# A four-layer graph network kernel: LSTM state laid batch-outer again, attention as a two-deep pipeline over groups

## The chip, the cores and the metric

The kernel runs on one core of a Trainium2 chip. The core has five engines that run side by side, each through its own queue: TensorE (PE for its matmuls, PEld for its weight loads), VectorE (DVE), ScalarE (ACT), GpSimd (POOL) and SyncE (SP, which only issues transfers here). They wait for each other through semaphores. The metric is the device time of one execution in microseconds (us). A profile gives, for one execution, the start and length of each instruction and the clock that was granted to TensorE, as a share of full speed.

## The reference

The input is x, 128 graphs of 64 nodes with 256 features in fp32: 8192 tokens. One 64x64 matrix adj serves all graphs. Four layers follow each other; each normalizes x over its features, applies ReLU, computes a function of the result and adds it to x.

```
layer 0: h = relu(adj (h Wg0 + bg0)); h = relu(adj (h Wg1 + bg1))
         for p in 1, 2, 3, 4:                    # windows of p nodes
             wins = h[:, : (64 // p) * p] as windows of p nodes
             h at the last node of each window = last hidden state of an
                 LSTM (weights of p, gates i, f, g, o) over the window
layer 1: attention with 4 heads of 64 features over the 64 nodes of a graph,
         scores masked where adj == 0
layer 2: normalized adj times h, two linear layers, each with a batch norm
layer 3: three graph convolutions with adj * adj, 256-512-1024-256
```

The four LSTMs run one after another, since each reads what the one before wrote into h.

## The kernel before

**Tiling.** The 8192 tokens are 16 groups of 512 (GN); x stays in SBUF in 16 tiles, xs[g], tokens on partitions. Matmuls are fp32; the program's records show two TensorE instructions for each written matmul (transposes one). All PSUM results go through one ring of eight banks (bank(), L49).

**Layer 0.** For each group (L192 to L209), the graph convolutions leave features on partitions, tokens along the free dimension. ScalarE writes the result into one of four resident tiles hs[i], each for 32 graphs (HB). A tile is [P, 2, NODES, HB]: the node is the outer index and the graph the inner one, so ScalarE reads its PSUM bank with a step of 64 elements (L207). The LSTM stage (L211 to L311) works on blocks of up to 512 windows, two blocks at a time. gate() (L222) multiplies the input of step t, read straight from hs (`win`, L218), and from step 1 on the hidden state `hid`, by the gate's weights, accumulates in one bank, and ScalarE applies sigmoid or tanh (L235). VectorE combines the gates into the cell (L245 to L250) and the new hidden state; at a window's last step the product is written back into hs (L258). What a matmul streams at step t is

```
hw = hs[i][:, :, k0 * p : (k0 + nk) * p, b0 : b0 + nb]
win = [hw[:, c].rearrange("p (k q) b -> p k q b", q=p) for c in range(2)]
... win[c][:, :, t, :]                  # runs of nb = 32 or 16 neighbours
```

to_residual (L269) first copies a group from hs into graph-outer order (hc; one half by POOL, one by VectorE, L275), then TensorE transposes it and VectorE adds it to x (L288). For the first two tiles this is issued in the middle of the LSTM with p = 4, for the other two after it.

**Layer 1.** For each group in turn (L319 to L409): ln_relu and to_features give hT; eight matmuls give queries and keys (L332, copied by ScalarE at L336), then values (L347, L353); 32 matmuls of 64x64 give the scores (L363); VectorE scales and masks them (L369), subtracts the maximum (L376, L377), ScalarE takes the exponential (L378), VectorE the sum and its reciprocal; TensorE transposes the result (L388), ScalarE copies it to eT (L391), 32 matmuls of 64x64 multiply it by the values (L399), VectorE divides by the sum (L406) and POOL adds to x (L409). A 64x64 matmul uses a quarter of the array: `par` selects the half of the rows (where its operands lie), `b` the half of the columns (where its output goes). In the loops of L356 to L362 and L393 to L398, par is the outermost index.

**Layers 2 and 3** follow with the lines L441 to L568; the change doesn't touch them.

**Order.** The program is written as above; a scheduler then puts each engine's instructions into one fixed queue, and may move some ahead, above all layer-norm statistics (L113, L115) of later groups. Engines take their queues strictly in order. Pools with bufs=2 let two groups' tiles live at the same time.

## Time and profile before

Median of three runs: 3057.72 us (3055.09 to 3057.88).

| | us |
|---|---|
| profiled execution, own time | 3057.72 |
| its span, first to last instruction | 3055.9 |
| TensorE matmul busy | 2908.4 (95%) |
| VectorE, ScalarE, POOL busy | 880.1, 860.4, 126.9 |
| mean TensorE clock | 0.964 |

Cut by stages, from the start of each to the start of the next:

| stage | from, us | length, us | TensorE clock |
|---|---|---|---|
| setup and graph convolutions | 0.0 | 234.9 | 1.00 |
| LSTM p=1 | 234.9 | 164.7 | 1.00 |
| LSTM p=2 | 399.6 | 302.0 | 1.00 |
| LSTM p=3 | 701.6 | 343.5 | 1.00 |
| LSTM p=4, half of the residual | 1045.1 | 381.6 | 1.00 |
| rest of the residual, first norm | 1426.7 | 17.2 | 1.00 |
| attention | 1443.9 | 407.6 | 0.77 |
| layer 2, first half | 1851.5 | 161.8 | 0.96 |
| layer 2, second half | 2013.3 | 145.7 | 0.96 |
| layer 3 | 2159.0 | 896.9 | 1.00 |

In the profile's lines L12 is line 12 of the kernel; a group names engine, operation, output<-inputs, shape and count, then busy time and mean length of one in ns, then the engine's idle time before it and what ended it. A matmul's length overlaps with the next one's, so the distance of starts says more than the length. "h" in a matmul of L230 is the tile hs, "hid" the hidden state.

### The profile page before, as it was taken

Reading aid. Unit: us, or ns where it says so; the run is one execution under the profiler, and the core shown is the slowest. Engines: PE = TensorE matmul, PEld = TensorE weight load, DVE = VectorE, ACT = ScalarE, POOL = GpSimd, SP = SyncE. Lnnn points to the kernel's source line nnn. Section 1 sums busy time; section 2 is a strip of 40 time slices with the busy share of each in tenths; the row PEclk is TensorE's granted clock in tenths of the full one; section 3 lists DMA queues with packets and bytes.
Section 4 is the critical chain, followed back from the end, with each engine's and each line's share of the span. In section 5 each row is a group of like instructions: output and inputs, shape, how many; then the busy total and the mean of one; then the engine's idle time right before and its main releaser. Section 6 shows DMA issues by size and latency. Waiting matters only on the chain.

```text
span 3055.9 us, 28553 instructions
## 1 busy us (share of the span) xinstructions
PE 2908.4 (95%) x12130; PEld 1727.2 (57%) x12130; DVE 880.1 (29%) x1789; ACT 860.4 (28%) x1435; POOL 126.9 (4%) x122
## 2 busy tenths in 40 slices
PE   7999999999999999999888888999999999999999
PEld 6784444446666544444555555544565656656656
DVE  5332222222222212434433435444521211111111
ACT  2324533333333322322323326260311111111111
POOL 1000000000000000101111112000000000000000
PEclk9999999999999999999777778999999999999999
DMA  5000000000000000000000000001000000000000
GB/s 163 1 1 0 1 14 0 1 0 28 1 1 1 14 0 0 0 0 25 1 1 1 1 1 1 0 1 48 1 14 7 14 7 7 14 7 8 14 7 14
DMA packets 23938, 32.35 MB, mean 11 GB/s; under 512 B 1281, under 2 KB 20225, under 8 KB 23809
## 3 DMA queue, kind: packets, MB, share of 16 engines
q1 hardware_dynamic: 22512, 29.63, 2.9%
q8 instruction: 95, 1.56, 0.2%
q10 hardware_dynamic: 1296, 0.89, 0.1%
q14 instruction: 35, 0.28, 0.0%
HBM read 22.13 MB, written 8.39 MB: 10 GB/s over the span
## 4 chain that ended last, share of the span: by engine, by line
PE 91%; DVE 4%; ACT 2%; POOL 1%; issue 1%; DMA 0%; ACTq 0%; POOLq 0%; DVEq 0%
PE ps L230 39%; PE ps L541 14%; PE ps L555 7%; PE ps L140 5%; PE ps L332 4%; PE ps L529 4%; PE ps L475 4%; PE ps L451 3%; PE ps L181 3%; PE ps L347 2%; PE ps L399 2%; PE ps L130 1%; PE ps L363 1%; PE ps L388 1%; PE ps L563 1%; POOL rstd L117 1%
## 5 line engine op out<-in xcount | busy, mean ns | idle before, releaser
L230 PE MATMUL ps<-h,w 128*128 128x512 f32 (+1 forms) x2016 | 809.1, 541 | 0.0
L230 PEld LDWEIGHTS ps<-h,w 128*128 128x128 f32 x2016 | 382.8, 190 | 377.5 <-issue 298.7
L230 PE MATMUL ps<-hid,w 128*128 128x512 f32 (+1 forms) x1152 | 466.3, 527 | 0.0
L541 PE MATMUL ps<-arena 128*128 128x512 f32 x1024 | 442.1, 592 | 0.0
L230 PEld LDWEIGHTS ps<-hid,w 128*128 128x128 f32 x1152 | 218.7, 190 | 199.5 <-issue 150.4
L541 PEld LDWEIGHTS ps<-arena 128*128 128x128 f32 x1024 | 193.3, 190 | 237.3 <-issue 236.5
L555 PE MATMUL ps<-arena 128*128 128x256 f32 x1024 | 223.6, 379 | 0.0
L555 PEld LDWEIGHTS ps<-arena 128*128 128x128 f32 x1024 | 194.6, 190 | 33.3 <-issue 7.7
L249 DVE TENSOR_TENSOR gi<-gi,gg 128x512 f32<-128x512 f32 (+1 forms) x72 | 43.9, 610 | 438.1 <-ACT gg L235 438.1
L235 ACT ACTIVATE gg<-ps,lbias 128x512 f32<-128x512 f32 (+1 forms) x144 | 91.9, 638 | 235.2 <-PE ps L230 235.2
L548 DVE TENSOR_SCALAR arena<-ps 128x512 f32<-128x512 f32 x64 | 44.3, 692 | 391.7 <-PE ps L541 391.7
L235 ACT ACTIVATE gi<-ps,lbias 128x512 f32<-128x512 f32 (+1 forms) x144 | 91.9, 638 | 219.4 <-PE ps L230 219.4
L546 ACT ACTIVATE arena<-ps 128x512 f32<-128x512 f32 x64 | 38.2, 597 | 404.5 <-PE ps L541 404.5
L332 PE MATMUL ps<-hT,wqk 128*128 128x512 f32 x256 | 133.7, 682 | 1.4 <-DVE rstd L116 1.4
L253 ACT ACTIVATE th<-c 128x512 f32<-128x512 f32 (+1 forms) x144 | 83.6, 581 | 157.3 <-DVE c L250 105.7
L451 PE MATMUL ps<-arena,w 128*128 128x512 f32 x256 | 116.5, 609 | 8.9 <-DVE arena L446 8.9
L475 PE MATMUL ps<-arena,w 128*128 128x512 f32 x256 | 112.8, 604 | 5.2 <-ACT arena L467 5.2
L529 PE MATMUL ps<-arena 128*128 128x512 f32 x256 | 115.0, 602 | 0.4 <-DVE arena L524 0.4
L245 DVE TENSOR_TENSOR c<-gi,gg 128x512 f32<-128x512 f32 (+1 forms) x72 | 46.9, 651 | 199.1 <-ACT gg L235 199.1
L117 POOL TENSOR_TENSOR rstd<-rstd,mhalf 128x4 f32<-128x4 f32 x64 | 64.5, 1008 | 891.7 <-DVE rstd L116 891.7
L140 PEld LDWEIGHTS ps<-wT,arena 128*128 128x128 f32 x768 | 93.3, 195 | 12.3 <-issue 7.7
L388 PE MATMUL ps<-ident,e 128*128 128x128 f32 x128 | 31.5, 428 | 71.0 <-ACT e L378 71.0
(114 smaller groups left out, 2629.5 us busy)
## 6 DMA issues: line engine op xcount, KB each, us to landing
x<-in_x SPq DMA_DIRECT2D x16, 512.0 KB, 9.1
out<-x SPq DMA_DIRECT2D x16, 512.0 KB, 2.9
w<-in_wih SPq DMA_DIRECT2D x4, 1024.0 KB, 8.7
w<-in_whh SPq DMA_DIRECT2D x3, 1024.0 KB, 5.7
arena<-in_l3w SPq DMA_DIRECT2D x3, 1024.0 KB, 5.0
wg<-in_wg ACTq DMA_DIRECT2D x2, 256.0 KB, 4.3
wqk<-in_wqkv SPq DMA_DIRECT2D x1, 512.0 KB, 3.7
w<-in_w1t SPq DMA_DIRECT2D x1, 512.0 KB, 4.9
```

What stands on the lines that cost most here:

```text
L117: nc.gpsimd.tensor_tensor(out=rstd, in0=rstd, in1=mhalf, op=ALU.pow)
L140: nc.tensor.matmul(ps[:, t * P : (t + 1) * P], lhsT=src[:, t, c * P : (c + 1) * P], rhs=rhs, start=True, stop=True,)
L181: nc.tensor.matmul(ps[:, t, :], lhsT=srcT[:, c, tok : tok + P], rhs=w[:, c, :], start=(c == 0), stop=(c == 1),)
L230: nc.tensor.matmul(o, lhsT=lhsT, rhs=rhs, start=(k == 0), stop=(k == len(ops) - 1))
L235: nc.scalar.activation(g[:, 0:n], ps, func, bias=lbias[:, col : col + 1])
L253: nc.scalar.activation(th[:, 0:n], cm, AF.Tanh)
L332: nc.tensor.matmul(ps, lhsT=wqk[:, c, col : col + P], rhs=hT[:, c, :], start=(c == 0), stop=(c == 1),)
L451: nc.tensor.matmul(ps, lhsT=w1[:, c, m * P : (m + 1) * P], rhs=a[:, 2 + c, :], start=(c == 0), stop=(c == 1),)
L475: nc.tensor.matmul(ps, lhsT=w2[:, c, m * P : (m + 1) * P], rhs=a[:, c, :], start=(c == 0), stop=(c == 3),)
L529: nc.tensor.matmul(ps, lhsT=a[:, 2 + c, t * P : (t + 1) * P], rhs=w31[:, c, :], start=(c == 0), stop=(c == 1),)
L541: nc.tensor.matmul(ps, lhsT=w32[k][:, c, m * P : (m + 1) * P], rhs=m1[:, c, :], start=(c == 0), stop=(c == 3),)
L555: nc.tensor.matmul(ps[:, t, :], lhsT=h2[c // 4][:, c % 4, tok : tok + P], rhs=w33[:, c, :], start=(c == 0), stop=(c == 7),)
```

## The change

Two parts. In layer 0, hs is [P, 2, HB * NODES]: the graph is the outer index and the node the inner one. The input of step t is then read, and the window's result written, with a step of p elements. hs is already in the order that the residual needs, so the copies hc are gone; the transposes and adds of all groups come after the last LSTM. ScalarE writes hs from PSUM in plain order. The blocks are cut by graphs alone; the numbers and sizes of the matmuls stay the same.

In layer 1 the body is cut into functions (features, queries_keys, values, softmax, turn, attend), and the loop runs one group ahead: the transposition of the softmax and the product with the values belong to the group before the one whose queries, keys, values and scores are computed. In both 64x64 passes par becomes the innermost index and each par has its own bank, so that consecutive matmuls use the four quarters of the array in turn.

```diff
-            hres.tile([P, 2, NODES, HB], F32, tag=f"h{i}", name=f"h{i}")
+            hres.tile([P, 2, HB * NODES], F32, tag=f"h{i}", name=f"h{i}")
...
-                        dst[:, c], ps.rearrange("p (b n) -> p n b", n=NODES), AF.Relu
+                mix(s1, adjT, 2, lambda c, ps: nc.scalar.activation(dst[:, c, :], ps, AF.Relu))
...
-                hw = hs[i][:, :, k0 * p : (k0 + nk) * p, b0 : b0 + nb]
-                win = [hw[:, c].rearrange("p (k q) b -> p k q b", q=p) for c in range(2)]
+                hb = hs[b0 // HB].rearrange("p c (b n) -> p c b n", n=NODES)
+                hb = hb[:, :, b0 % HB : b0 % HB + nb, 0 : nw * p]
+                win = [
+                    hb[:, c].rearrange("p b (k q) -> p b k q", q=p) for c in range(2)
+                ]
...
-                    ops = [(wi[:, c, col : col + P], win[c][:, :, t, :]) for c in range(2)]
+                    ops = [(wi[:, c, col : col + P], win[c][:, :, :, t]) for c in range(2)]
...
-            def to_residual(i):
-                    hc = lp.tile([P, 2, GB, NODES], F32, tag="hc", name="hc")
-                    for c, eng in enumerate((nc.gpsimd, nc.vector)):
-                        eng.tensor_copy(
-                            hc[:, c], hs[i][:, c, :, b0 : b0 + GB].rearrange("p n b -> p b n")
-                        )
...
-            for p, nk, nb in ((1, 16, 32), (2, 16, 32), (3, 21, 16), (4, 16, 32)):
+            for p, nb in ((1, 8), (2, 16), (3, 16), (4, 32)):
...
-                        if p == 4 and j == 2 and t < 2:
-                            to_residual(t)
-            for i in range(2, len(hs)):
-                to_residual(i)
+            for g in range(NG):
+                per = HB * NODES // GN
+                hsrc, o = hs[g // per], (g % per) * GN
+                for k in range(2):
...
+            pss = [bank((P, 2 * GT, NODES)) for _ in range(2)]
+            for t in range(GT):
+                for m in range(2):
                     for b in range(2):
                         tok = t * P + b * NODES
-                        for m in range(2):
+                        for par in range(2):
+                            rows = slice(par * 64, par * 64 + 64)
                             nc.tensor.matmul(
-                                ps[b * 64 : b * 64 + 64, 2 * t + m, :],
+                                pss[par][b * 64 : b * 64 + 64, 2 * t + m, :],
...
+        last = None
+        for g in range(NG + 1):
+            if g < NG:
+                hT = features(g)
+                q, k = queries_keys(hT)
+            if last is not None:
+                e, ri, v_last = last
+                eT = turn(e)
+            if g < NG:
+                v = values(hT)
+            if last is not None:
+                attend(g - 1, eT, v_last, ri)
+            if g < NG:
+                last = (*softmax(q, k), v)
```

## The prediction

> **What bounds the kernel now.** I first cut the span into stages (the busy time by stretches; columns: stretch, its length, busy time and instructions of PE, PEld, DVE, ACT, POOL, then granted clock, DMA share, GB/s):

> ```profile
> 399.60:701.60 302.00, 302.00 (x705) 133.72 (x704) 65.50 (x97) 95.56 (x145) 0.00 (x0) 1.00 0.01 4
> 701.60:1045.10 343.50, 343.50 (x1217) 231.02 (x1216) 80.06 (x160) 115.54 (x224) 0.00 (x0) 1.00 0.02 6
> 1045.10:1426.70 381.60, 378.77 (x929) 170.87 (x929) 106.69 (x201) 101.71 (x153) 15.04 (x13) 1.00 0.01 3
> ...
> 1443.90:1851.50 407.60, 336.41 (x3576) 242.11 (x3576) 160.33 (x317) 121.99 (x202) 54.78 (x47) 0.77 0.01 4
> ```

> The first three are the LSTMs of window 2, 3 and 4: TensorE is busy without a gap at full clock, so every nanosecond added to a matmul there is added to the time. The last is attention: TensorE idles 71 us, and its clock averages 0.77. Next I read one attention group in TensorE's timeline (start, length):

> ```profile
> 1489.74 3.27 PE L399 MATMUL ps<-v,eT 64*64 64x64 f32 x62
> 1492.94 1.97 PE L130 MATMUL ps<-ident,h 128*128 128x128 f32 x8
> 1494.83 8.98 PE L332 MATMUL ps<-hT,wqk 128*128 128x512 f32 x16
> 1503.74 3.76 PE L347 MATMUL ps<-wv,hT 128*64 128x128 f32 x64
> 1507.43 2.00 PE L363 MATMUL ps<-k,q 64*64 64x64 f32 x64
> 1513.88 1.97 PE L388 MATMUL ps<-ident,e 128*128 128x128 f32 x8 [4.45 <-ACT e L378]
> 1515.78 3.43 PE L399 MATMUL ps<-v,eT 64*64 64x64 f32 x64
> ```

> The wait of 4.45 us is for the softmax, and it costs a second time: the same 64 matmuls take 2.00 us before it (L363) and 3.43 us after it (L399). Stretches cut at these passes show clock 0.50 for L388, L399 and L130 and 1.00 for L347 and L363. Groups alternate between 25.0 and 26.2 us, 25.6 on average. Last, the groups by form, for what strided reads show:

> ```profile
> L230 PE MATMUL ps<-h,w 128*128 128x512 f32 x1312 | 589.3, 592 | 0.0
> L230 PE MATMUL ps<-h,w 128*128 128x336 f32 x704 | 219.8, 446 | 0.0
> ...
> L275 POOL COPY hc<-h 128x512 f32<-128x512 f32 x16 | 18.8, 1201 | 1248.9 <-DVE h L258 1123.3 <-PE ps L284 125.6
> ...
> L275 DVE COPY hc<-h 128x512 f32<-128x512 f32 x16 | 8.9, 598 | 0.1
> ```

> A matmul's 592 ns includes overlap; the spacing is what counts. In the timeline four 128x512 records start every 1.715 us (429 ns each) and four 128x336 every 1.13 us (282 ns). Check: the 384+704 records of windows 1 and 2 times 429 ns are 466.7 us, exactly their stretch, and 1216 times 282.5 ns are the 343.5 us of window 3. One element passes each 0.84 ns. L275 is the only element-wise strided SBUF read on VectorE (step 128 bytes).

> [...]

> **Part A, the LSTM layout.** Instruction counts and sizes are unchanged. The moving operand's inner step becomes p elements (L225): 4 bytes at p=1, 8 at p=2, 12 at p=3, 16 at p=4. Only the input product (names h,w) is affected; hid stays contiguous. Records: 384 at p=1, 448 at p=2, 704 at p=3, 480 at p=4. TensorE's price is unknown and bounded thus. Low end 0[...]. Middle[...]. Then p=2[...] costs nothing; p=3 touches three lines per four elements[...], 433 against 282 ns; p=4 costs 880 against 429 ns. That is 704 x 0.149 = 105 plus 480 x 0.447 = 214, together **+319 us**. High end:[...] p=2 pays 448 x 0.447 = 200 and p=3 704 x 0.293 = 206, together +620. I take the middle[...]. Nothing hides it, TensorE being full.

> VectorE's last products (L258) now write with the same steps. At most 40 of them, 0.69 us each, may take twice as long; VectorE is under 30% busy there, so this hides under the matmuls, except for the last, some 0.5 us.

> **Part B, the residual after the LSTM.** Gone: 16 POOL and 16 VectorE copies (L275), and 2.8 us in which TensorE waited for them inside window 4. But all 128 transposes and 32 adds (L288) now stand after the last LSTM matmul. Adds bind: 32 x 0.625 = 20 us, done 21.5 us after that matmul; stats, aggregate, rstd on POOL (1.0), relu: 4.5; remaining relus, transposes, copies to hT: 3.5. First query matmul at 29.5. Before: 17.2, plus the 64 transposes (7.6 us) and 2.8 us of waiting inside window 4, is 27.6. **+2 us.**

> **Part C, the pipeline.** The queued order is now: turn (the transposes of L388) of group g-1 after queries/keys of g, then values, attend of g-1, scores of g. Before each score evacuation VectorE has nothing late; after it, it copies the two halves of the next hT with the maximum between. From the end of scores, by the durations above at full clock:
> - two e (1.50), first hT half (0.69): 2.4; maximum (1.22), second half (0.69): 4.4. TensorE has transposes (0.96, half of 1.97) and two records in that time, so it idles some 2.5 us, in two pieces, below what cost it the clock before.
> - 14 more L332 records at 0.429: 10.4. The softmax is done at 6.7 (subtract 1.23, exponential 1.06), so turn doesn't wait: 11.4.
> - values 3.7: 15.1; attend and scores, 64 records each, 30.5 ns now at full clock. Going round four quarters[...] 1.6 us each: 18.3. If rotation brings nothing, 19.0.

> 14 cycles x (25.6 - 18.3) = **-102 us**. The first two groups gain nothing: VectorE has some 19 us of statistics for later groups queued ahead of the first e, which holds the scores' readers until about 48 us after the LSTM where scores end at 44. The last group drains as before.

> Sum against the profiled span: 3055.9 + 319 + 2 - 102 = 3274.9. The profiled execution's own time is 1.8 above its span and is also the median of the three runs, so **3277 us**.

> **Rivals.**
> - *TensorE doesn't mind the step (faster).* Part A costs 0: 3057.7 + 2 - 102 = 2958 us. For it: TensorE streams at 0.84 ns per element[...], so a line per element may be just enough; ScalarE reads PSUM with a 256-byte step at L206 (595 ns) as quickly as contiguously at L200 (594).[...] It decides at p=4: if p=3 is free, break-even is a record of 429 + 100/0.48 = 637 ns, 1.24 ns per line.
> - *Only 16 bytes pays.*[...] 3277 - 105 = 3172 us.
> - *The pair rule.* p=2 and p=3 pay in full: 3277 + 301 = 3578 us.
> - *The pipeline gives little.* VectorE's order (maximum ahead of the second hT half) or the ring of eight PSUM banks leaves cycles at 22 us: a gain of 50, so 50 us more in each case above.

> **How the numbers follow.** Full line cost 0.31 (3277); no cost 0.27 (2958); only p=4 0.22 (3172); pair rule or worse 0.14 (3578); a smaller mixture, mostly under 100 us, 0.06. A difference within 0.2%, 6 us, is no more than measurements of this kernel tell from no change. Faster 0.27 and a little of the mixture, 0.29; same 0.02; slower 0.69. The range 2945 to 3330 leaves out only the pair rule and a few worse tails. The likeliest's own range, with the pipeline at 75 to 115 us, is 3235 to 3330.

> **What would show it.** The h,w records' spacing: 429 ns at p=1 and p=2, 433 at p=3, 880 at p=4, beside unchanged hid records. Window 4's stretch should grow by 211, window 3's by 105. In attention: clock near 1.0, cycles near 18.3, no wait of the turn (L388) for the exponential. Wrong if p=4 records stay at 429, if p=2 records lengthen, or if the clock stays at 0.5 behind each score pass.

## The result and the profile after

The changed kernel takes **3274.17 us** (median of four runs, 3272.86 to 3277.01), beside 3057.03 us for the kernel before in the same comparison: a ratio of 1.0712 (95% interval 1.0694 to 1.0731), 217 us slower. The predicted time was 3277 us. The total hides two errors of about 35 us with opposite signs, so the parts have to be read one by one.

The first view is again the busy time by stretches, now of the kernel after (stretch, length, busy time and instructions of PE, PEld, DVE, ACT, POOL, then clock, DMA share, GB/s), cut where the LSTMs with p = 2, 3 and 4, the residual and attention begin:

```profile
399.30:710.60 311.30, 311.30 (x705) 132.44 (x704) 65.43 (x97) 95.66 (x145) 0.00 (x0) 1.00 0.01 4
710.60:1172.70 462.10, 462.10 (x1217) 236.20 (x1216) 81.29 (x160) 118.72 (x225) 0.00 (x0) 1.00 0.01 5
1172.70:1769.40 596.70, 596.70 (x865) 172.31 (x864) 79.42 (x112) 102.52 (x152) 0.00 (x0) 1.00 0.01 2
1769.40:1797.75 28.35, 18.89 (x137) 14.75 (x135) 25.94 (x62) 4.24 (x8) 2.01 (x2) 0.87 0.21 66
1797.75:2067.60 269.85, 240.18 (x3576) 165.91 (x3576) 155.02 (x357) 118.63 (x203) 54.79 (x47) 0.97 0.01 2
```

TensorE is busy throughout the three LSTM stretches, as before, with as many instructions, and yet they are longer: 302.0 has become 311.3, 343.5 has become 462.1. Window 4 before was 381.6 us, of which some 370.7 were its 864 matmul records and 10.9 half of the residual; it is now 596.7 without any residual. Attention went from 407.6 to 269.85 us and its clock from 0.77 to 0.97.

| part | predicted | measured in the profiles |
|---|---|---|
| LSTM p=2 | 0 | 311.3 - 302.0 = +9.3 |
| LSTM p=3 | +105 | 462.1 - 343.5 = +118.6 |
| LSTM p=4 | +214 | 596.7 - 370.7 = +226.0 |
| residual | +2 | 28.35 - 17.2 - 10.9 = +0.3 |
| attention | -102 | 269.85 - 407.6 = -137.8 |

These add up to +216.4, and the spans differ by 217.0 (3272.9 and 3055.9).

The matmuls that became longer are those that read hs. TensorE's timeline of the kernel after at p = 3 and at p = 4 (start, length of the merged stretch; it is the distance of starts that counts):

```profile
799.73 1.97 PE L227 MATMUL ps<-h,w 128*128 128x336 f32 x4
801.53 1.30 PE L227 MATMUL ps<-hid,w 128*128 128x336 f32 x4
802.67 1.97 PE L227 MATMUL ps<-h,w 128*128 128x336 f32 x4
...
1400.22 1.90 PE L227 MATMUL ps<-hid,w 128*128 128x512 f32 x4
1401.96 3.76 PE L227 MATMUL ps<-h,w 128*128 128x512 f32 x4
1405.54 1.90 PE L227 MATMUL ps<-hid,w 128*128 128x512 f32 x4
```

At p = 3 four h records take 1.80 us and four hid records, of the same size but contiguous, 1.14: 450 and 285 ns each. At p = 4 it is 3.58 and 1.73 us: 895 and 433 ns. The same reading at p = 2 (502.13 to 503.93 us) gives 450 against 429 ns, and at p = 1 the records stay at 429.

Attention, one group of the kernel after in TensorE's timeline (L393 is the product with the values, L350 the scores, L313 the queries and keys, L379 the transposition of the softmax):

```profile
1835.54 7.11 PE L313 MATMUL ps<-hT,wqk 128*128 128x512 f32 x16 [1.20 <-DVE hT L131]
1842.48 1.04 PE L379 MATMUL ps<-ident,e 128*128 128x128 f32 x8
1843.44 3.76 PE L330 MATMUL ps<-wv,hT 128*64 128x128 f32 x64
1847.14 1.16 PE L393 MATMUL ps<-v,eT 64*64 64x64 f32 x64
1848.12 1.11 PE L350 MATMUL ps<-k,q 64*64 64x64 f32 x64
1849.16 1.09 PE L128 MATMUL ps<-ident,h 128*128 128x128 f32 x8
1851.58 0.67 PE L313 MATMUL ps<-hT,wqk 128*128 128x512 f32 x1 [1.32 <-DVE hT L131]
```

The wait for the exponential is gone. What is left is 1.3 us per group before the query and key matmuls, for the copy to hT. A cycle is 1851.58 - 1835.54 = 16.04 us, against 25.6 before. The pass with the values takes 0.98 us from its start to the next start, where it had been 3.36. The scores' pass takes 1.04 us; as a stretch it is 1.11 us long and was 2.00.

### The profile page after: what moved, and what is told of

Same layout as the page of the kernel before. It is cut to its first block, busy times and chain, and to the rows that moved or that the text cites. A ratio compares the mean times of both kernels' runs of the same rounds, so it can differ in the third digit from the quotient of the medians.

```text
span 3272.9 us, 28518 instructions
## 1 busy us (share of the span) xinstructions
PE 3165.4 (97%) x12130; PEld 1662.9 (51%) x12130; DVE 858.6 (26%) x1773; ACT 860.9 (26%) x1435; POOL 107.7 (3%) x106
## 4 chain that ended last, share of the span: by engine, by line
PE 91%; DVE 5%; ACT 2%; POOL 1%; issue 0%; DMA 0%; ACTq 0%; POOLq 0%; DVEq 0%
PE ps L227 47%; PE ps L552 13%; PE ps L566 7%; PE ps L138 4%; PE ps L540 3%; PE ps L486 3%; PE ps L313 3%; PE ps L462 3%; PE ps L179 2%; PE ps L330 2%; POOL rstd L115 1%; PE ps L574 1%; DVE st L111 1%; ACT h L118 1%; PE ps L393 1%; DVE x L288 1%
## 5 line engine op out<-in xcount | busy, mean ns | idle before, releaser
L227 PE MATMUL ps<-h,w 128*128 128x512 f32 (+1 forms) x2016 | 1162.3, 721 | 0.0
L227 PEld LDWEIGHTS ps<-h,w 128*128 128x128 f32 x2016 | 390.7, 194 | 587.8 <-issue 546.0
L313 PE MATMUL ps<-hT,wqk 128*128 128x512 f32 x256 | 117.1, 611 | 25.1 <-DVE hT L131 25.1
L232 ACT ACTIVATE go<-ps,lbias 128x512 f32<-128x512 f32 (+1 forms) x144 | 91.1, 633 | 96.6 <-PE ps L227 94.4
L232 ACT ACTIVATE gf<-ps,lbias 128x512 f32<-128x512 f32 (+1 forms) x72 | 44.8, 623 | 231.8 <-PE ps L227 231.8
```

Source lines behind the costliest of these rows:

```text
L227: nc.tensor.matmul(o, lhsT=lhsT, rhs=rhs, start=(k == 0), stop=(k == len(ops) - 1))
L232: nc.scalar.activation(g[:, 0:n], ps, func, bias=lbias[:, col : col + 1])
L313: nc.tensor.matmul(ps, lhsT=wqk[:, c, col : col + P], rhs=hT[:, c, :], start=(c == 0), stop=(c == 1),)
```

## The experiments

**One part at a time.** The first question was whether the two parts are what they seem: each was taken alone, by joining the layer 0 of one kernel to the attention of the other.

The pipeline alone is the kernel before with the whole of the change in layer 1, the round of the four quarters included; these are its first and last lines:

```diff
-        for g in range(NG):
+        def features(g):
             h = ap_.tile([P, GT, D], F32, tag="h", name="h")
             ln_relu(xs[g], h)
             hT = ap_.tile([P, 2, GN], F32, tag="hT", name="hT")
             to_features(h, hT)
+            return hT
...
+        last = None
+        for g in range(NG + 1):
```

> The layout of before with the pipelined attention. If the two parts add up, attention falls from 407.6 to about 270 us as in the changed kernel and the LSTM stages stay at 164.7, 302.0 and 343.5 us: 3057 - 137 = 2920 us. Rival: part of the attention's gain was owed to the new layout (group 0's statistics, residual order); then the attention stage stays above 280 us and the time above 2930 us.

Measured: 2913.70 us, ratio 0.9535 (0.9521 to 0.9549), 141 us faster.

The layout alone is the kernel before with the change in layer 0:

```diff
-            hres.tile([P, 2, NODES, HB], F32, tag=f"h{i}", name=f"h{i}")
+            hres.tile([P, 2, HB * NODES], F32, tag=f"h{i}", name=f"h{i}")
...
-                    ops = [(wi[:, c, col : col + P], win[c][:, :, t, :]) for c in range(2)]
+                    ops = [(wi[:, c, col : col + P], win[c][:, :, :, t]) for c in range(2)]
```

> The layout of the changed kernel with the attention of before. If the two parts add up: LSTM 1535 us instead of 1181 without its residual, attention near 408 us: 3274 + 137 = 3411 us. Rival: the two parts interact (statistics or residual adds that now collide with attention): off by more than 10 us from 3411.

Measured: 3415.23 us, ratio 1.1177 (1.1160 to 1.1194), 360 us slower. The two differences, +360.1 and -141.4 against their common reference of 3055.12, add up to +218.7, and the change as a whole is +217.1. So the parts hardly interact. In the pipeline alone, attention takes 261.5 us rather than 269.85, since there the statistics of the first groups are done earlier (the second group's matmuls wait 0.97 us for hT, and 5.43 us in the changed kernel) and the first group runs at full clock (its query and key matmuls take 7.03 us, and 8.59 in the changed kernel). This is where it beat its expectation by 6 us.

**What a strided read costs TensorE.** Three prices had to be told apart: one for every line (a line is here 16 bytes of SBUF, counted from the tile's start), one for every element outside an aligned pair (the prediction's pair rule), one by the step. The 450 ns at p = 2, where no two streamed words are neighbours, already speak against the second; but the changed kernel varies lines and step together. So the next kernel streams runs of two neighbouring words, placed differently at each window size.

```diff
+# per window size: first word, words in a run, words from run to run
+PATTERNS = {2: (1, 2, 4), 3: (0, 2, 6), 4: (3, 2, 8)}
...
+                    off, run, hop = PATTERNS[p]
+                    v = flat[:, c, 0 : n // run * hop].rearrange("p (r s) -> p r s", s=hop)
+                    return v[:, :, off : off + run]
...
-                    ops = [(wi[:, c, col : col + P], win[c][:, :, :, t]) for c in range(2)]
+                    ops = [(wi[:, c, col : col + P], src(c, t)) for c in range(2)]
```

> The changed kernel with other words streamed into the input products (the LSTMs compute with other inputs; counts and sizes stay): p=2 runs of two words, words 1 and 2 of each four; p=3 words 0 and 1 of each six; p=4 words 3 and 4 of each eight, which lie on both sides of a line's border. If a 16-byte line costs about 1.75 ns whatever is read of it: p=2 450 ns per record (one line per pair), p=3 295 ns, p=4 895 ns (each word its own line), total about 3274 - 704 x 0.155 = 3165 us. If only pairs that start on an 8-byte border run at full speed: p=2 and p=4 895 ns, p=3 283 to 295 ns, about 3360 us. If the step of the innermost dimension decides (4 bytes everywhere): 429, 283 and 429 ns, about 2930 us.

Measured: 3164.41 us in its one run, beside 3165 by the line rule. TensorE's timeline of this kernel at p = 3 and at p = 4:

```profile
875.69 1.34 PE L243 MATMUL ps<-h,w 128*128 128x336 f32 x4
876.87 1.29 PE L243 MATMUL ps<-hid,w 128*128 128x336 f32 x4
877.99 1.34 PE L243 MATMUL ps<-h,w 128*128 128x336 f32 x4
...
1301.15 1.90 PE L243 MATMUL ps<-hid,w 128*128 128x512 f32 x4
1302.88 3.76 PE L243 MATMUL ps<-h,w 128*128 128x512 f32 x4
1306.46 1.90 PE L243 MATMUL ps<-hid,w 128*128 128x512 f32 x4
```

At p = 3 four h records take 1.18 us, 295 ns each; at p = 4 3.58 us, 895 ns each; at p = 2 they stand at 450 ns. All three are what the line rule gives. The aligned-pair rule falls with p = 2, whose pairs start off an 8-byte border and cost no more than a step of two words does; a rule by the step falls with p = 4, where neighbouring words that lie on both sides of a line's border cost as much as words 16 bytes apart.

The next kernel asks whether the distance between lines counts, and whether a broken run costs anything by itself.

```diff
-PATTERNS = {2: (1, 2, 4), 3: (0, 2, 6), 4: (3, 2, 8)}
+PATTERNS = {2: (0, 4, 8), 3: (0, 3, 4), 4: (0, 1, 8)}
...
+                    if p == 4:
+                        line = flat[:, c].rearrange("p (r s) -> p r s", s=hop)[:, :, off]
+                        return line.unsqueeze(1).to_broadcast([P, 2, n // 2])
```

> The changed kernel with other words streamed into the input products (the LSTMs compute with other inputs; counts and sizes stay): p=2 runs of four words on a line, every second line; p=3 three words of each four; p=4 one word of each eight, 32 bytes apart, swept twice. If a line costs 1.75 ns however far the next one is: 429 ns (four words per line), 283 ns, 895 ns, total 3274 - 9 - 118 = 3147 us. Rival, the step's size matters beyond 16 bytes[...]: p=4 above 895 ns[...]. Rival, any break in the run costs: p=2 and p=3 above 429 and 283 ns.

Measured: 3154.07 us in its one run. Its timeline at p = 4:

```profile
1299.15 3.83 PE L246 MATMUL ps<-h,w 128*128 128x512 f32 x4
1302.80 1.90 PE L246 MATMUL ps<-hid,w 128*128 128x512 f32 x4
1304.54 3.83 PE L246 MATMUL ps<-h,w 128*128 128x512 f32 x4
```

Four records take 3.65 us, 912 ns each: 32 bytes apart costs 2% more than 16. So the size of the step counts, as that rival says, but little; larger distances were not run. That the words are swept twice is not the cause: the kernel after this one sweeps words 16 bytes apart four times, and its records start every 0.90 us, as they do inside a run of four of the changed kernel. These 17 ns on 480 records are 8 us, the miss against the expectation. Runs of four on every second line stand at 429 ns (1.71 us for four, at p = 2), and three words of each four at 283 ns: in these two patterns, of 128 and 112 lines per record, a broken run costs nothing.

The last of this group measures whether the price belongs to TensorE's clock. In the attention of before, the first 1.4 to 3.8 us of a group's query and key matmuls run at half clock (0.50 from 1521.04 to 1522.40 us and, one group earlier, from 1494.83 to 1498.6); there they were made to stream one word of each line.

```diff
+            sparse = [
+                hT[:, c].rearrange("p (r s) -> p r s", s=4)[:, :, 0]
+                .unsqueeze(1).to_broadcast([P, 4, GN // 4])
+                for c in range(2)
+            ]
...
-                            ps, lhsT=wqk[:, c, col : col + P], rhs=hT[:, c, :],
+                            ps.rearrange("p (a r) -> p a r", a=4),
+                            lhsT=wqk[:, c, col : col + P], rhs=sparse[c],
```

> The kernel before, with the query and key matmuls streaming one word of each 16-byte line of hT, swept four times (the attention computes with other queries and keys). The first some 4 us of these matmuls run at half clock in every group, the rest at full clock. If the time per line belongs to the memory and not to TensorE's clock: all 16 records stand at 895 ns. If it is counted in TensorE's cycles: 895 ns at full clock, twice that, 1790 ns, at half clock. Total for the first: 16 x 0.895 = 14.3 us instead of 7.7 to 8.9 per group, 3057 + 16 x 6.0 = 3153 us; for the second about 1.8 us more per group, 3182 us.

Measured: 3158.69 us in its one run. TensorE's timeline, one group:

```profile
1505.67 1.97 PE L130 MATMUL ps<-ident,h 128*128 128x128 f32 x8
1507.57 14.75 PE L337 MATMUL ps<-hT,wqk 128*128 128x512 f32 x16
1522.24 3.77 PE L353 MATMUL ps<-wv,hT 128*64 128x128 f32 x64
```

The 16 records take 1522.24 - 1507.57 = 14.67 us. The next view has first the stretch of this group that ran at half clock (the third number from the end), then weight loads, one of which starts with each record from the second on:

```profile
1507.57:1510.20 2.63, 2.63 (x4) 1.11 (x4) 0.86 (x2) 2.08 (x4) 0.27 (x2) 0.50 0.00 0
...
1508.63 0.31 PEld L337 LDWEIGHTS ps<-hT,wqk 128*128 128x128 f32 x1 [0.57 <-DVE hT L133]
1509.54 0.31 PEld L337 LDWEIGHTS ps<-hT,wqk 128*128 128x128 f32 x1 [0.59 <-issue]
1510.43 0.21 PEld L337 LDWEIGHTS ps<-hT,wqk 128*128 128x128 f32 x1 [0.59 <-issue]
```

The second record, at half clock, takes 0.90 us, and so does each of those that follow at full clock (1510.43 is the start of the fourth); only the first takes 1.07 us. Counted in TensorE's cycles, the second would have taken 1.79 us. So the time per line is not counted in TensorE's cycles. The half clock covered less of these matmuls than the "some 4 us" of the expectation, here 2.6 us, but that doesn't change the reading.

All together, with the lines that a record touches:

| read | lines per record | ns per record | ns per line |
|---|---|---|---|
| p=4, one word per line (mean of a run of four) | 512 | 895 | 1.75 |
| p=3, step 12 bytes, every line of 16 rows of 64 words | 256 | 450 | 1.76 |
| p=2, step 8 bytes | 256 | 450 | 1.76 |
| words 1 and 2 of each four | 256 | 450 | 1.76 |
| words 0 and 1 of each six | 168 | 295 | 1.76 |
| words 3 and 4 of each eight | 512 | 895 | 1.75 |
| one word of each eight | 512 | 912 | 1.78 |
| four words of each eight | 128 | 429 | bound by 512 elements |
| three words of each four | 112 | 283 | bound by 336 elements |

In all nine patterns a record takes the larger of 0.84 ns for each element and about 1.76 ns for each line that it enters. So two words of each line still cost 450 instead of 429 ns, and one word 895, while at three words of each line nothing is lost (283 ns for 336 elements).

**The round of the four quarters.** The prediction put it at 0.35 us per pass; the passes show more. First the changed kernel with only the old order inside the passes:

```diff
-            for t in range(GT):
-                for m in range(2):
-                    for b in range(2):
-                        for par in range(2):
-                            rows = slice(par * 64, par * 64 + 64)
+            for par in range(2):
+                rows = slice(par * 64, par * 64 + 64)
+                for t in range(GT):
+                    for b in range(2):
+                        for m in range(2):
...
```

> The changed kernel, but both 64x64 passes keep the row half (par) as the outermost index, so that only two quarters of the array alternate. If the round of four quarters is what brings a pass from 1.95 to about 1.0 us: both passes return to 1.95, about 1.9 us more per group, 3274 + 15 x 1.9 = 3303 us. Rival: the passes are short because of the full clock and fuller queues alone: passes stay near 1.0 us and the time at 3274 us.

Measured: 3284.14 us, ratio to the kernel before 1.0751 (1.0733 to 1.0769); only 10 us more than the changed kernel. TensorE's timeline of this kernel:

```profile
1846.90 1.83 PE L393 MATMUL ps<-v,eT 64*64 64x64 f32 x59
...
1848.70 1.83 PE L350 MATMUL ps<-k,q 64*64 64x64 f32 x59
1850.45 1.09 PE L128 MATMUL ps<-ident,h 128*128 128x128 f32 x8
1851.99 7.11 PE L313 MATMUL ps<-hT,wqk 128*128 128x512 f32 x16 [0.45 <-DVE hT L131]
```

Two passes take 3.55 us, 1846.90 to 1850.45, instead of 2.02: the round does shorten them, by 1.5 us. But the wait that follows is 0.45 us instead of 1.32. With par outermost, one bank is complete halfway and VectorE starts on it, and so comes earlier to the copy that TensorE waits for. 0.9 of the 1.5 us are given back there. The expectation failed on both: it put a pass at 1.95 us, where it takes 1.78, and it counted the passes alone.

Then the round alone, in the kernel before, with nothing pipelined; the edit is that of the change in these loops.

> The kernel before, with only the order inside the two 64x64 passes changed to the round of four quarters, nothing pipelined. The scores' pass should fall from 1.95 to about 1.04 us, the one with the values, at half clock, from 3.36 to about 2.0: 2.3 us per group. But both score banks are then complete only at the pass's end, while before VectorE began on the first bank 0.76 us earlier; since everything there is in series, about 0.7 us comes back. Net 1.6 us x 16: 3057 - 26 = 3031 us. Rival, nothing comes back: 3057 - 37 = 3020 us.

Measured: 3014.06 us, ratio 0.9864 (0.9847 to 0.9880), 42 us faster; better than both expectations. Its timeline, one group:

```profile
1499.37 1.16 PE L363 MATMUL ps<-k,q 64*64 64x64 f32 x64
1505.58 1.97 PE L389 MATMUL ps<-ident,e 128*128 128x128 f32 x8 [5.06 <-ACT e L379]
1507.48 1.99 PE L400 MATMUL ps<-v,eT 64*64 64x64 f32 x64
1509.40 1.95 PE L130 MATMUL ps<-ident,h 128*128 128x128 f32 x8
1511.46 7.13 PE L332 MATMUL ps<-hT,wqk 128*128 128x512 f32 x16
1518.53 3.71 PE L347 MATMUL ps<-wv,hT 128*64 128x128 f32 x63
```

The passes are shorter as expected, and the wait for the softmax is 0.6 us longer, as expected (5.06 against 4.45). What was not expected is L332: 7.07 us here, full speed, against 7.7 to 8.9 before. That is the other 1.2 us per group. The granted clock (third number from the end) shows why. Two stretches of the kernel before, the first from the end of the pause:

```profile
1513.88:1522.40 8.52, 8.52 (x82) 7.21 (x83) 4.22 (x6) 2.34 (x5) 2.54 (x2) 0.50 0.01 2
1522.50:1529.00 6.50, 6.50 (x19) 2.68 (x19) 2.12 (x10) 2.66 (x6) 1.01 (x1) 1.00 0.00 0
```

The same two of this kernel:

```profile
1505.58:1511.20 5.62, 5.62 (x80) 4.94 (x80) 3.13 (x5) 1.17 (x2) 0.91 (x1) 0.50 0.01 3
1511.25:1518.50 7.25, 7.14 (x17) 2.96 (x16) 2.95 (x12) 3.82 (x7) 2.56 (x3) 1.00 0.00 0
```

The half clock itself became shorter. Over all groups but the last it ended 8.4 to 10.9 us after the pause in the kernel before and 3.0 to 5.6 us after it here, though the pause here is the longer one. So the full clock does not come back a fixed time after the pause. The two kernels differ in the order of the 64x64 matmuls, and thus in how densely they follow each other; which property of the work brings the clock back sooner was not separated.

**The wait that is left.** Of the pipelined cycle 1.3 us are idle, while VectorE evacuates the scores (reads them out of PSUM) and only then copies the next hT. Two kernels move the next group's norm and transposes ahead, on the layout of before. The first places them ahead of the values product:

```diff
+        hT = features(0)
...
             if g < NG:
                 v = values(hT)
+            if g + 1 < NG:
+                hT = features(g + 1)
             if last is not None:
                 attend(g - 1, eT, v_last, ri)
```

> The layout of before with the pipelined attention, and the next group's norm, transposes and copies to hT moved ahead of the values product of the group before, so that VectorE copies hT before the scores are due. If TensorE's 1.3 us of idleness per group comes from the copies to hT being queued behind the score evacuation, it vanishes: cycle 16.05 - 1.3 = 14.7 us, 2914 - 15 x 1.3 = 2894 us. Rival: the wait moves to the softmax (evacuation, maximum, subtraction and exponential take 5.0 us against 6.9 us of query and key matmuls) or to ScalarE: the time stays near 2914 us.

Measured: 2924.54 us, ratio 0.9569 (0.9554 to 0.9583): 11 us worse than the pipeline alone. Its timeline around one set of scores:

```profile
1488.91 1.11 PE L372 MATMUL ps<-k,q 64*64 64x64 f32 x64
1489.95 7.13 PE L335 MATMUL ps<-hT,wqk 128*128 128x512 f32 x16
...
1491.59 1.23 DVE L118 SCALAR_TENSOR_TENSOR nmr<-mv,rstd 128x4 f32<-128x4 f32 x1
...
1493.26 0.75 DVE L113 BATCH_NORM_STATS2 st<-x 128x6 f32<-128x256 f32 x2
1493.93 1.27 DVE L379 SCALAR_TENSOR_TENSOR e<-ps,mask 128x512 f32<-128x512 f32 x2
...
1499.31 1.09 PE L401 MATMUL ps<-ident,e 128*128 128x128 f32 x8 [2.23 <-ACT e L388]
```

The query matmuls now follow the scores at once, but VectorE, which had the scores complete at 1489.95, does the division, the next norm and statistics first and evacuates them 4 us later. The softmax ends late and TensorE waits 2.2 us for it: the rival's outcome. Place and queue order, not the length of the softmax, are to blame, as the other place shows:

```diff
             if last is not None:
                 attend(g - 1, eT, v_last, ri)
+            if g + 1 < NG:
+                hT = features(g + 1)
             if g < NG:
                 last = (*softmax(q, k), v)
```

> The layout of before with the pipelined attention, and the next group's transposes placed between the values product and the scores, where VectorE's queue keeps the score evacuation ahead of the next norm. If the copies to hT ahead of the scores are what removes the 1.3 us, and the wait that came up with the features further ahead was owed to statistics queued ahead of the evacuation: the softmax ends about 6.2 us after the scores, before the 6.9 us of query and key matmuls are over, cycle 14.8 us, 2914 - 15 x 1.3 = 2895 us. Rival, the softmax chain is too long for this order in any case: it ends later than the matmuls and the time stays at 2910 us or above.

Measured: **2895.37 us**, ratio 0.9477 (0.9461 to 0.9493), the fastest of all. Its timeline:

```profile
1485.26 1.16 PE L372 MATMUL ps<-k,q 64*64 64x64 f32 x64
...
1486.39 7.10 PE L335 MATMUL ps<-hT,wqk 128*128 128x512 f32 x16
1487.56 0.17 DVE L116 TENSOR_SCALAR rstd<-mv 128x4 f32<-128x4 f32 x1 [0.72 <-ACT h L120]
1487.64 1.28 DVE L379 SCALAR_TENSOR_TENSOR e<-ps,mask 128x512 f32<-128x512 f32 x2
...
1493.33 1.04 PE L401 MATMUL ps<-ident,e 128*128 128x128 f32 x8
```

The evacuation starts 1.3 us after the scores' end, the exponential ends at 1492.6, and the transposes of it follow the query matmuls without a wait. A cycle is 14.85 us. One small step of the next norm (L116) still stands ahead of the evacuation, and VectorE idles 0.72 us for it; TensorE no longer waits for that.

## Why the prediction was right, and where its sum was not

**What bounds the stages** was right: TensorE stays full in the LSTMs and every nanosecond of its matmuls arrived in the time. The two single-part kernels show it without the other part. One figure beside it needs care: the clock of the graph convolutions, 1.00 in the table of stages. Just ahead of them stands a gap of 8.64 us, and 2.9 us after its end their first 16 matmuls of 128x256 take 6.27 us, where the later ones take 3.72. That column alone does not prove full speed there.

**Part A** took the middle of its prices, 880 ns for a record of 512 lines. The trace of before did not show that price: VectorE's strided copy there (L275) takes 598 ns for 512 elements. That TensorE pays by the line is shown by the two pattern kernels, and the price was 2% low (895 ns). The term was mis-sized by 35 us, 354 for 319: p = 2 was counted at nothing although its 256 lines at that price are 440 ns, already above the 429 of a contiguous stream; it costs 450 - 429 = 21 ns on 448 records, 9.4 us. p = 3 and 4 cost 450 and 895 ns rather than 433 and 880, which is another 12 and 7 us; the sum also took 447 for 880 - 429 = 451 ns and 149 for 433 - 282 = 151, together 3 us. The hid records are 2 to 4 ns slower than before, some 3 us. By the prediction's own sign ("Wrong if ... p=2 records lengthen") the free step of two words is refuted: they lengthened by 5%, far less than the pair rule asks. The low end (TensorE doesn't mind the step), the pair rule and "only 16 bytes pays" are all refuted: p = 3 pays 118.6 us.

VectorE's strided products, counted as hidden, take 0.69 us at 8 bytes, 0.61 instead of 0.51 at 12 and 1.07 instead of 0.69 at 16, and nothing waited for them that can be seen in the LSTM stretches.

**Part B** was right: 28.35 us from the last LSTM matmul to the first query matmul, predicted 29.5.

**Part C** was mis-sized by 36 us, the other way. Two steps of the cycle failed. The passes that go round the four quarters were taken at "1.6 us each", which the trace of before did not show; they take 1.04 and 0.98 us, 15 to 16 ns per record: 1.2 us per cycle. "maximum (1.22), second half (0.69): 4.4", with TensorE pausing "in two pieces": in the compiled queue the first-half products of three banks (six records, 2.6 us) stand ahead of the first one that needs the second half, so TensorE paused once, for 1.3 us, and not for 2.5; 1.1 us per cycle. 14 cycles of 2.3 us are 32 us. The rest is group 1, which was to gain nothing on 25.6 us: its scores ended 22 us after those of group 0. The 138 us also lie outside the 75 to 115 us that the likeliest case allowed the pipeline. The clock stayed up behind the short pauses, as predicted (1.00 over the cycles from 1835.54 to 1883.6 us, each with a pause of 1.3 us); the statistics ahead of the first evacuation held it up, as predicted, for 5.4 us of TensorE's time in group 1.

That the total came within 3 us of the median is therefore partly luck: the mechanisms were right, and two sizes were off by a tenth (A) and a third (C) in opposite directions.

## What to carry to other kernels

Count the 16-byte lines that a matmul's moving operand enters, not only its elements: here fp32 lost 5% at two words per line (450 for 429 ns), and at one word per line the matmul took twice as long (895 ns), which no other engine's idleness hides when TensorE is the bound. When passes become shorter, look at which bank is complete when: finishing two banks together can give back on VectorE what it gained on TensorE, here 0.9 of 1.5 us. In a software pipeline the place of the next stage's preparation decides what the in-order queues put ahead of the critical evacuation; moving it by one step was worth 29 us here.
